# Layer 0 of a four-layer graph network: update and normalization of finished rows as steps of a scheduled list

## The chip, the cores and the metric

The kernel runs on one core of a Trainium2 chip. The metric is the device time of one execution in microseconds (us). The engines are called as the profile calls them: PE (TensorE), DVE (VectorE), ACT (ScalarE), POOL (GpSimd), SP (SyncE, which issues most DMAs); PEld is PE's loading of weights.

## The reference, cut to what matters

Four graph layers, each followed by a residual and a layer normalization. Only layer 0 is changed. N = 2708 nodes, D = 128; `adj` is 2708 x 2708, symmetric in its pattern and about 2.3% dense.

```python
def _L0_gnn_ref(node_feats, adj, msg_w, msg_b, upd_w, upd_b, ln_w, ln_b):
    s = node_feats @ msg_w[:, :D].T
    d = node_feats @ msg_w[:, D:].T
    messages = gelu(s[:, None, :] + d[None, :, :] + msg_b)       # exact gelu
    aggregated = jnp.einsum('ijd,ij->id', messages, adj)
    combined = jnp.concatenate([node_feats, aggregated], axis=-1)
    new_feats = combined @ upd_w.T + upd_b
    h = gelu(new_feats) + node_feats
    mu, var = jnp.mean(h, -1, keepdims=True), jnp.var(h, -1, keepdims=True)
    return (h - mu) / jnp.sqrt(var + LN_EPS) * ln_w + ln_b
...
x = _layernorm(x + _L0_gnn_ref(x, adj, ...))   # layer 0
x = _layernorm(x + _L1_gnn_ref(x, adj, adj, ...))
x = _layernorm(x + _L2_gnn_ref(x, adj, ...))
x = _layernorm(x + _L3_gnn_ref(x, adj, ...))
```

So each row of layer 0's result needs the aggregate of that row, one product with the second half of `upd_w`, a gelu, and two normalizations in a row. Every row is independent of the others.

## The kernel before, in words

Layer 0 does not compute all pairs. For each row tile of 125 rows (22 of them, `Rows`) and each of 22 column blocks of up to 124 columns, it finds the nonzero entries of `adj`: a mask on DVE, ranks by a product with a triangular matrix on PE, and 0/1 matrices `S` on DVE, one for each rank up to five. A block then is: `begin` and `pick` on PE (gather s + d and the weights by products with `S` into a bank `sl`), a gelu on ACT into `g`, the weights `W` on DVE (`weigh`), and `add_up` on PE, which sums weighted messages into the bank `acc`. There are 484 blocks. Entries beyond rank five are "far": DVE finds their places (`max`, `max_index`), POOL gathers rows of a table by indirect DMA (L992, 14 for each row tile), ACT applies gelu and weights to them, and DVE adds them to `extra`. When a row tile is through, `turn` on PE and `close` on ACT write its aggregate, transposed, into columns of `aggT`. `aggT` held x transposed until layer 0's products with x were made.

All of this is a list of steps. `Order.add` takes an engine, an estimated cost, what a step reads and writes, and a due time in blocks (table `DUE`). `Order.run` walks a clock and on each engine takes, of the steps whose inputs are there, the one due first; a step of another kind than the last one on PE counts as due `STAY` blocks later, which keeps alike products together. The order that comes out is each engine's program; on the chip each engine runs it in order and waits where an input is missing. `prepare` (the tables of s, d and of u, which is x's part of the update, stored in `u_tab`) belongs to the same list. One PSUM bank, `misc`, is taken and given back by the steps that need it (ranks, `turn`).

After the list the rest of layer 0 is written out by hand (class `Update` and the lines behind `order.run`): one load of all of u into `o` (`load`, L1156); in groups of four tiles of 128 rows the product with `upd_a` (L1167), the add, gelu (L1169), the residual (L1174), `moments` (L417) and POOL's x + ln_b (L1176); then `Resnorm`: in two halves of 11 tiles, `normalizer` (small operations of 128x11 on DVE and a square root on ACT, L365), a scaling of each tile (`shift`: ACT L455, DVE L457), the product with ln_w (L474), the residual (L475), statistics again, a second `normalizer` and scaling. ACT's square root needs another table than gelu, which costs a table load. Layer 1 then transposes x (L1353), and multiplies it (L1356, L1365, L1359).

Of the kernel before, what the change touches and what calls it, by code (L numbers as in the profile page):

```python
# [15 lines left out]
F32 = mybir.dt.float32  # L16
BF16 = mybir.dt.bfloat16
U32 = mybir.dt.uint32
AF = mybir.ActivationFunctionType
ALU = mybir.AluOpType  # L20
AX = mybir.AxisListType
# [2 lines left out]
P = 128  # L24
BANK = 512
# [12 lines left out]
def spans(start, stop, step):  # L38
    return [(a, min(a + step, stop)) for a in range(start, stop, step)]
# [41 lines left out]
class Order:  # L81
# [4 lines left out]

    LATENCY, TURN, STAY = 0.12, 0.1, 42.0

    def __init__(self):
        self.steps, self.wrote, self.read = [], {}, {}
# [156 lines left out]
def gnn_stack(ctx: ExitStack, tc: tile.TileContext, t, out: bass.AP):  # L249
# [164 lines left out]
    def moments(st, src, a, b):  # L414

        for i in range(a, b):
            nc.vector.bn_stats(out=st[:, i, :], in_=src[:, i, :])  # L417
# [100 lines left out]
    def sums(dst, a, b, r, terms, psum, bias):  # L518

        ps = psum.tile([P, BANK // D, D], F32, name="ps")  # L520
        for i in range(a, b):
            for k, (src, w) in enumerate(terms):
                nc.tensor.matmul(ps[:r, i - a, :], src[:, i * P:i * P + r], w,  # L523
                                 start=k == 0, stop=k == len(terms) - 1)
        nc.vector.tensor_tensor(dst, ps[:r, :b - a, :], over_tiles(bias, b - a, r), op=ALU.add)  # L525
# [103 lines left out]
    with ExitStack() as l0:  # L629
# [10 lines left out]
        with ExitStack() as msg:  # L640
# [79 lines left out]
            def columns_of(sl, a, b):  # L720
# [4 lines left out]

            xT = aggT
            order = Order()
            DUE = {"piece": 0, "spread": -10, "s_out": 23.5, "d_out": 37, "u": 25, "load": -125, "load_s": 94.5,
                   "load_row": -58.5, "start_far": 206, "rank": -20, "rank_row": -18.5, "begin": -1.8, "pick": 0.5,
                   "add_up": 3, "turn": 34.5, "out": 57.5, "cast": -58.5, "a_hi": 21, "gelu": -9.5, "far_weigh": 97.5,  # L730
                   "close": 113.5, "far_gelu": 106, "weigh": -63.5, "largest": -8.5, "index": -35, "mask": -10,
                   "far_sum": -34, "past": -77, "max": -4.5, "a_lo": -12, "S": 4, "fetch": 211}
            add = order.add
            assert NC == 5 and NB % 4 == 2

# [116 lines left out]
            class Rows:  # L852
# [111 lines left out]
                def add_far(self, first):  # L964
# [11 lines left out]
                    for n in range(NOV):  # L976
# [12 lines left out]
                        for k in range(min(8, OV - 8 * n)):  # L989

                            def fetch(k=k, far=far, ix=ix):
# [4 lines left out]
                            add("POOL", 1.95, fetch, due + DUE["fetch"] + k,  # L996
                                reads=[("ix", f), ("far", f), *(("d_tab", j) for j in range(6))],
                                writes=[("far", f, k)], lag=4.0)
                        if t == LT - 1 and n == NOV - 1:
                            break  # L1000
                        self.add_far_gelu(n, f, due)
                    if t < LT - 1:
                        add_, tail = add, self.far_sums(fars)
                        for engine, cost, emit, reads, writes in tail:
                            add_(engine, cost, emit, first + DUE["far_sum"], reads=reads, writes=writes)
                    self.fars = fars

                def add_far_gelu(self, n, f, due):
                    w = min(8, OV - 8 * n)
# [28 lines left out]
                def add_turn(self, due):  # L1038
                    one = ("misc", self.t, "turn")
                    add("PE", 0.85, self.turn, due + DUE["turn"], reads=[("extra", self.t % 2), "agg", "spread"], writes=[one],  # L1040
                        lag=0.08, take="misc", kind="all")
                    add("ACT", 0.2, self.close, due + DUE["close"], reads=[one],
                        writes=[("xT", k) for k in range(len(spans(0, NT, 4)))], give=("misc", one, 1))

                def turn(self):

# [100 lines left out]
                        reads=[("v", t, n) for t in range(LT) for n in range(NOV)]  # L1147
                        + [("count", t, m) for t in range(LT) for m in range(-(-NB // PB))])

            class Update:  # L1150

                def load(self):
                    self.new = o_all[:, :NT * D].rearrange("p (n d) -> p n d", d=D)
                    nc.sync.dma_start(out=self.new, in_=u_tab.rearrange("(n p) d -> p n d", p=P))  # L1156

                def open(self):
                    room, V = (Values.within(g_all[(LT * NB + k) % 6].rearrange("p a d -> p (a d)")) for k in range(2))
                    self.st = room.part([P, NT, 6])  # L1160
                    self.norm = Resnorm(self.new, x, ln_w, self.st, room.part([P, NT, 6]), V)

                def sums(self, n):
                    a, b, r = groups()[n]
                    g, ps = self.new[:r, a:b, :], sl_all[n % 3][:r, n // 3 % 2, :].rearrange("p (i d) -> p i d", d=D)
                    for i in range(a, b):
                        nc.tensor.matmul(ps[:, i - a, :], aggT[:, i * P:i * P + r], upd_a, start=True, stop=True)  # L1167
                    nc.vector.tensor_tensor(g, g, ps[:, :b - a, :], op=ALU.add)
                    nc.scalar.activation(g, g, AF.Gelu)  # L1169

                def rows(self, n):
                    a, b, r = groups()[n]
                    g = self.new[:r, a:b, :]
                    nc.vector.tensor_tensor(g, g, x[:r, a:b, :], op=ALU.add)  # L1174
                    moments(self.st, self.new, a, b)
                    nc.gpsimd.tensor_tensor(x[:r, a:b, :], x[:r, a:b, :], over_tiles(ln_b, b - a, r), op=ALU.add)  # L1176

            U = Update()
            turn_x()
            for n in range(len(spans(0, NB, 4))):  # L1180
                prepare(n)
            for n, (engine, load) in enumerate((
                    ("SP", side_by_side), ("SP", lambda: weight("L1_gnn_W_q")), ("SP", lambda: weight("L1_gnn_W_k")),
                    ("SP", lambda: weight("L1_gnn_W_upd", P)), ("SP", lambda: column("L1_gnn_b_msg")),
                    ("SP", lambda: weight("L3_gnn_W")), ("POOL", lambda: across("L1_gnn_gate_bias")),
                    ("POOL", lambda: across("L1_gnn_ln_gamma")), ("POOL", lambda: across("L1_gnn_ln_beta")),
                    ("POOL", lambda: across("L2_gnn_att_b")), ("POOL", lambda: across("L3_gnn_b")))):
                add(engine, 0.55, load, (5 + n) * NB, reads=[("far", 0, 0)])
            R = [Rows(i) for i in range(LT)]
            for row in R:  # L1190
                row.add()
                row.add_blocks()
                if row.t < LT - 1:
                    row.add_turn(row.t * NB)
            add("DVE", 0.2, lambda: nc.vector.tensor_copy(
                spread[:, :, :RG], ident[:, R[-1].used].rearrange("p (c i) -> p c i", c=NC)), (LT - 1) * NB + 10,
                writes=["spread"])
            add("SP", 0.1, U.load, (LT - 1) * NB + 7, reads=[("u_tab", n) for n in range(6)],
                writes=[("o", m) for m in range(-(-NB // PB))], lag=6.0)
            add_check((LT - 1) * NB + 8)  # L1200
            with tc.manual_schedule():
                order.run({"misc": 1})

                def last_gelu():
                    R[-1].far_gelu(NOV - 1)

                def far_sums():
                    for k in range(OV - 8 * (NOV - 1)):
                        R[-1].far_weigh(NOV - 1, k)
                    for _, _, emit, _, _ in R[-1].far_sums(R[-1].fars):  # L1210
                        emit()

                G = len(groups())
                ahead = LR * (LT - 1) // BANK
                U.open()
                for n in range(ahead):
                    U.sums(n)
                    if n > 0:
                        U.rows(n - 1)
                    if n == 1:  # L1220
                        last_gelu()
                    if n == 2:
                        far_sums()
                R[-1].turn()
                R[-1].close()
                U.rows(ahead - 1)

                ones = mp.tile([P, 1], F32, name="ones")
                fine = mp.tile([P, LT], F32, name="fine")
                n_fine = mp.tile([P, 1], F32, name="n_fine")  # L1230
                nc.vector.memset(ones, 1.0)
                nc.vector.tensor_tensor(fine, tot[:, :, 0], tot[:, :, 1], op=ALU.add)
                nc.vector.tensor_tensor(fine, fine, fine, op=ALU.is_equal)
                nc.vector.tensor_reduce(n_fine, fine, AX.X, ALU.add)
                nc.vector.scalar_tensor_tensor(most, most, float(LT), n_fine, op0=ALU.add, op1=ALU.subtract)

                def between():
                    ps = misc
                    nc.tensor.matmul(ps[:1, 0, :1], ones, most, start=True, stop=True)
                    for n in range(ahead, G):  # L1240
                        U.sums(n)
                    nc.vector.tensor_copy(bad_n, ps[:1, 0, :1])
                    for n in range(ahead, G):
                        U.rows(n)

                U.norm.all(between)

    def all_pairs():

# [862 lines left out]
```

## Time and profile before

| | us |
|---|---|
| runs | 1790.2, 1800.12, 1800.02 |
| median | 1800.02 |
| profiled execution: its own time | 1797.42 |
| profiled execution: span from first to last instruction | 1795.6 |
| PE busy | 1531.0 (85%) |
| DVE busy | 1342.2 (75%) |
| ACT busy | 1069.3 (60%) |
| POOL busy | 566.1 (32%) |

All durations come from the one profiled execution. A line of the profile gives a start, a duration, an engine, the line of the kernel, the operation, output<-input by the program's names, and in brackets how long the engine was idle before and what ended that idle time. A busy share is an average over stages with different limits, so the stages have to be read one by one. The profile says of itself that the ends of matmuls are modelled, and that spans on POOL are rough.

### The profile page before, as it was taken

To read this page: it belongs to the slowest core of one execution; us is meant where nothing else is said; L and a number is where in the kernel's file an instruction comes from. 1 tells how busy PE (TensorE), PEld (TensorE's weight loads), DVE (VectorE), ACT (ScalarE), POOL (GpSimd) and SP (SyncE) were. 2 spreads that over 40 slices of the span, in tenths; PEclk is the share of its full clock that TensorE was granted. 3 is DMA by queue.
4 is the path that set the end of the run, shared out by engine and by line. 5 is a ranking of instruction groups with operands and counts; after the bars stand their busy time and mean duration, and the time that the engine had idled before them with its cause. 6 is when DMAs were issued, how large, how long until landed. Compare 5 with 4: busy or idle time off the path is not lost.

```text
span 1795.6 us, 36325 instructions
## 1 busy us (share of the span) xinstructions
PE 1531.0 (85%) x14033; PEld 936.3 (52%) x14033; DVE 1342.2 (75%) x3139; ACT 1069.3 (60%) x1846; POOL 566.1 (32%) x377
## 2 busy tenths in 40 slices
PE   5799999999999999954999993678887994499995
PEld 4577777777777777742444442222222442145442
DVE  6799999999999999965788858658886873851004
ACT  3378788787887878853453435668877743421003
POOL 2187767767777677641000000000000000000000
PEclk8799999999999999976999996679998996599998
DMA  8676776767767677422244400304334546153431
GB/s 188 167 147 137 166 150 145 153 138 168 145 140 163 145 161 151 103 45 93 99 157 153 157 3 0 113 32 145 145 125 139 171 130 266 65 217 124 155 129 33
DMA packets 228917, 236.37 MB, mean 132 GB/s; under 512 B 25522, under 2 KB 213654, under 8 KB 222146
## 3 DMA queue, kind: packets, MB, share of 16 engines
q1 hardware_dynamic: 184030, 213.15, 38.7%
q0 software_dynamic: 44704, 20.80, 9.9%
q8 instruction: 112, 1.84, 0.4%
q14 instruction: 71, 0.58, 0.1%
HBM read 218.74 MB, written 15.15 MB: 130 GB/s over the span
## 4 chain that ended last, share of the span: by engine, by line
PE 38%; DVE 7%; ACT 7%; issue 1%; ACTq 0%; DVEq 0%
PE acc L2009 11%; PE lg L1397 6%; PE acc L1404 6%; PE accV L1737 5%; PE ps L1665 3%; PE accO L1741 2%; PE ps L1720 1%; ACT arena L1671 1%; PE ps L1666 1%; DVE arena L1699 1%; ACT arena L1692 1%; DVE arena L1723 1%; ACT x L455 1%; PE ps L523 1%; PE ps_w L1365 1%
## 5 line engine op out<-in xcount | busy, mean ns | idle before, releaser
L992 POOL DMA_INDIRECT far<-d_tab,ix x308 | 517.1, 1679 | 251.1 <-ACT g L145 157.0
L145 ACT ACTIVATE g<-sl 128x640 f32<-128x640 f32 x484 | 335.8, 708 | 120.6 <-PE sl L1106 93.8
L1106 PE MATMUL sl<-dA,S 124*128 124x153 f16 x4840 | 378.8, 232 | 1.9 <-DVE S L908 1.9
L1106 PEld LDWEIGHTS <-S 124*128 124x128 f16 x4840 | 329.6, 98 | 47.2 <-issue 39.9
L1114 PE MATMUL acc<-g,W 128*32 128x128 f32 x4840 | 162.5, 275 | 0.7 <-DVE W L1123 0.6
L1098 PE MATMUL sl<-s,same 50*128 50x459 f16 (+1 forms) x968 | 144.4, 331 | 15.9 <-DVE W L1123 11.4
L1398 ACT ACTIVATE w<-lg,row_L_gnn_gate_bias 128x512 f32<-128x512 f32 (+1 forms) x132 | 83.5, 636 | 108.2 <-PE lg L1397 107.0
L1123 DVE TENSOR_TENSOR W<-sl,own 128x125 f32<-128x125 f32 x484 | 128.6, 278 | 16.6 <-ACT g L145 14.5
L1114 PEld LDWEIGHTS acc<-g,W 128*32 128x32 f32 x4840 | 125.8, 109 | 22.4 <-issue 10.9
L981 DVE FIND_INDEX8 ix<-v,o 128x8 uint32<-128x2728 f32 x44 | 131.7, 2994 | 0.0
L1652 POOL TENSOR_TENSOR arena<-arena,off 128x128 f32<-128x128 f32 (+1 forms) x22 | 22.2, 1010 | 340.4 <-DMA arena<-in_adjT 266.9
L1737 PE MATMUL accV<-arena,X 128*128 128x512 f32 (+4 forms) x264 | 123.4, 587 | 6.5 <-DVE arena L1703 6.5
L908 DVE TENSOR_SCALAR S<-rk 124x1000 f16<-124x1000 bf16 (+1 forms) x330 | 125.5, 430 | 0.4 <-ACT rk L888 0.4
L1397 PE MATMUL lg<-qT,mT 128*128 128x512 f32 (+2 forms) x264 | 121.2, 547 | 3.7 <-ACT w L1398 3.1
L1404 PE MATMUL acc<-w,both 128*128 128x512 f32 (+2 forms) x264 | 121.2, 547 | 0.0
L525 DVE TENSOR_TENSOR g<-ps,row_L_gnn_b 128x512 f32<-128x512 f32 (+2 forms) x14 | 8.0, 574 | 147.1 <-PE ps L523 147.1
L1665 PE MATMUL ps<-XT 128*128 128x512 f32 (+8 forms) x150 | 84.1, 647 | 32.2 <-ACT arena L1671 26.5
L2009 PE MATMUL acc<-at,x 128*128 128x512 f32 (+2 forms) x156 | 66.2, 574 | 48.5 <-ACT x L455 48.5
L1022 ACT ACTIVATE far<-far,v 128x128 f32<-128x128 f32 x308 | 104.1, 406 | 0.0
L927 DVE SCALAR_TENSOR_TENSOR o<-misc,ar 128x496 f32<-128x496 f32 x132 | 82.6, 626 | 28.0 <-PE misc L923 13.0
L1399 DVE TENSOR_TENSOR w<-w,at 128x512 f32<-128x512 f32 (+1 forms) x132 | 82.6, 625 | 27.1 <-ACT w L1398 27.1
L888 ACT CAST rk<-misc 124x512 bf16<-124x512 f32 x132 | 72.2, 547 | 44.8 <-PE misc L885 44.2
(359 smaller groups left out, 2502.7 us busy)
## 6 DMA issues: line engine op xcount, KB each, us to landing
at<-in_adjT SPq DMA_DIRECT2D x42, 1354.0 KB
ar<-in_adj SPq DMA_DIRECT2D x110, 248.0 KB
far<-s_tab SPq DMA_DIRECT2D x44, 512.0 KB
at<-in_adjT SPq DMA_DIRECT2D x44, 448.0 KB
arena<-in_adjT SPq DMA_DIRECT2D x21, 704.0 KB
arena<-in_adjT SPq DMA_DIRECT2D x21, 650.0 KB
held<-in_adjT SPq DMA_DIRECT2D x7, 1354.0 KB
f_tab<-arena SPq DMA_DIRECT2D x10, 704.0 KB
```

The source lines that it names most:

```text
L145: s.emit()
L981: add("DVE", 3.0, lambda n=n, ix=ix: nc.vector.max_index(ix, v[:, n * 8:n * 8 + 8], o_all[:, :NB * JB]), due + DUE["index"], reads=[("v", ...
L992: nc.gpsimd.indirect_dma_start(out=far[:, k, :], out_offset=None, in_=d_tab[:, :], in_offset=bass.IndirectOffsetOnAxis(ap=ix[:, k:k + 1], ...
L1098: nc.tensor.matmul(columns_of(sl, 0, DA)[:, a:e, :], same[p], self.s3[p, :e - a, :], start=True, stop=False)
L1106: nc.tensor.matmul(columns_of(sl, 0, DA)[:, c, :], S_all[h][:, n, c, :], dA[q][:, b, c, :], start=False, stop=q == 1 and c in (2, NC - 1))
L1114: nc.tensor.matmul(acc_all[q:q + 32, k, :], W_all[W][:, c, :], g_all[g][:, c, :], start=b == 0 and k == 0, stop=ends)
L1123: nc.vector.tensor_tensor(W[:, :, :RG], columns_of(sl, D, DA), own[:, None, :].to_broadcast([P, NC, RG]), op=ALU.mult)
L1397: nc.tensor.matmul(lg, mT[:, j * P:j * P + r], qT[:, a:b], start=True, stop=True)
L1404: nc.tensor.matmul(acc[k], mrow[:rows[j], j, :], ws[j][:rows[j], a:b], start=j == 0, stop=j == NT - 1)
L1665: nc.tensor.matmul(ps, XT[:, self.js], XT[:, c], start=True, stop=False)
L1737: nc.tensor.matmul(Pair.acc[0][:, a:b], X[:self.r, self.j, :], self.w_[:, a:b], start=first, stop=last)
L2009: nc.tensor.matmul(acc[k], src[:rows[j], j, :], at[:rows[j], a:b], start=j == order[0], stop=j == order[-1])
```

## The change: what it does

The update and both normalizations become steps of the list, by groups of finished row tiles of 128 rows: tiles 0 to 7 once row tile 8 is through, 8 to 15 after row tile 16, 16 to 19 after 20, 20 and 21 after 21 (`SETTLED`, `settle`). Their data lie in columns of `aggT` that are not in use at that time, u is loaded in four parts, and the products go through `misc`. The reciprocal root comes from an integer estimate on DVE and three Newton steps on POOL (`better`, four small operations each; `offset` is one more), so ACT needs no square root. The product with ln_w moves from DVE to POOL, and all scalings are on ACT. The last row tile's far gelu, far sums, `turn` and `close` and the check (`add_bad`) are steps of the list too. `close` now names only the banks of `aggT` that it writes. The due times of all steps and `STAY` are set anew.

```diff
-    LATENCY, TURN, STAY = 0.12, 0.1, 42.0
+    LATENCY, TURN, STAY = 0.12, 0.1, 64.0
...
-            DUE = {"piece": 0, "spread": -10, "s_out": 23.5, "d_out": 37, "u": 25, "load": -125, "load_s": 94.5,
...
+            DUE = {"piece": -5.5, "spread": -4.5, "s_out": 6, "d_out": 26, "u": 8.5, "settle": 25.5, "load": -145.5,
...
-            class Update:
...
-                def sums(self, n):
...
-                def rows(self, n):
...
+            def settle(a, b, room, few, due):
+                w, name = b - a, ("new", a)
+                area, held = columns(room, w * D)
+                T = area.rearrange("p (n d) -> p n d", d=D)
+                area, more = columns(few, w * 14)
+                st = area[:, :6 * w].rearrange("p (n k) -> p n k", k=6)
+                d, q, m, v, y, o, z, u = (area[:, k * w:(k + 1) * w] for k in range(6, 14))
+                even, odd, m2, m5 = (st[:, :, k] for k in (1, 4, 2, 5))
...
+                def load():
+                    nc.sync.dma_start(out=T, in_=u_tab[a * P:b * P, :].rearrange("(n p) d -> p n d", p=P))
...
+                for i, e, r in pieces:
...
+                    step("PE", 1.07 * share, sums, reads=[("xT", i * P // BANK)], writes=[one], lag=0.08, take="misc",
+                         kind="all")
+                    step("DVE", 0.1 + 0.5 * share, lambda t=t, ps=ps, r=r: tt(t[:r], t[:r], ps[:r], op=ALU.add), reads=[one],
+                         writes=[key], give=("misc", one, 1))
+                    step("ACT", 0.1 + 0.5 * share, lambda t=t: nc.scalar.activation(t, t, AF.Gelu), writes=[key])
+                    step("DVE", 0.1 + 0.5 * share, lambda t=t, i=i, e=e: tt(t, t, x[:, i:e, :], op=ALU.add),
+                         reads=[("x", i)], writes=[key])
+                    step("POOL", 0.1 + 1.2 * share, lambda i=i, e=e: nc.gpsimd.tensor_tensor(
+                        x[:, i:e, :], x[:, i:e, :], over_tiles(ln_b, e - i), op=ALU.add), writes=[("x", i)])
...
+                def rates():
+                    r, off = y, o
+                    def begin():
+                        tt(d, even, odd, op=ALU.subtract)
+                        stt(q, d, 0.25, d, op0=ALU.mult, op1=ALU.mult)
+                        stt(m, m2, LN_EPS * D, m5, op0=ALU.add, op1=ALU.add)
+                        stt(u, even, -1.0, odd, op0=ALU.mult, op1=ALU.subtract)
+                    def guess():
+                        stt(v, m, 1.0 / D, q, op0=ALU.mult, op1=ALU.add)
+                        nc.vector.tensor_scalar(y.bitcast(I32), v.bitcast(I32), -0.5, float(0x5f3759df), op0=ALU.mult,
+                                                op1=ALU.add)
+                        nc.vector.tensor_scalar(u, u, 0.5, None, op0=ALU.mult)
+                    def better():
+                        nc.gpsimd.tensor_tensor(z, v, y, op=ALU.mult)
+                        nc.gpsimd.tensor_tensor(z, z, y, op=ALU.mult)
+                        nc.gpsimd.tensor_scalar(z, z, -0.5, 1.5, op0=ALU.mult, op1=ALU.add)
+                        nc.gpsimd.tensor_tensor(y, z, y, op=ALU.mult)
...
+                    step("DVE", 0.7, begin, writes=[(name, "st"), *keys])
+                    step("DVE", 0.5, guess, writes=[(name, "st")])
+                    for _ in range(3):
+                        step("POOL", 0.9, better, writes=[(name, "st")])
+                    step("POOL", 0.25, offset, writes=[(name, "st"), *keys])
+                def scale(src, i, e, key):
+                    for k in range(i, e, 2):
...
+                        step("ACT", 0.39 * min(2, e - k), shift, reads=[(name, "st")], writes=[key])
+                for i, e, _ in pieces:
+                    look(lambda c: T[:, c - a, :], i, e, (name, i))
+                rates()
+                for i, e, _ in pieces:
+                    t, share = T[:, i - a:e - a, :], (e - i) / 4
+                    scale(lambda c: T[:, c - a, :], i, e, (name, i))
+                    step("POOL", 0.1 + 1.2 * share, lambda t=t, i=i, e=e: nc.gpsimd.tensor_tensor(
+                        t, t, over_tiles(ln_w, e - i), op=ALU.mult), writes=[(name, i)])
+                    step("DVE", 0.1 + 0.5 * share, lambda t=t, i=i, e=e: tt(x[:, i:e, :], x[:, i:e, :], t, op=ALU.add),
+                         reads=[(name, i)], writes=[("x", i)])
+                    look(lambda c: x[:, c, :], i, e, ("x", i))
+                rates()
+                for i, e, _ in pieces:
+                    scale(lambda c: x[:, c, :], i, e, ("x", i))
...
+            SETTLED = {8: (0, 8, 3 * BANK, 5 * BANK), 16: (8, 16, 0, 5 * BANK), 20: (16, 20, 2 * BANK, 0),
+                       21: (20, NT, BANK, BANK + 2 * P)}
             for row in R:
                 row.add()
                 row.add_blocks()
...
+                row.add_turn(row.t * NB)
+                if row.t in SETTLED:
+                    settle(*SETTLED[row.t], (row.t + 1) * NB + DUE["settle"])
...
             with tc.manual_schedule():
                 order.run({"misc": 1})
...
-                U.norm.all(between)
```

`look` emits the statistics (`bn_stats`) of two tiles as one step on DVE; the due time of each step in `settle` is 0.1 block later than that of the one before it.

## The prediction

> **What bounds the kernel now.** I cut the span into stages with the table of busy time by stretch:
>
> ```profile
> core 0: us, PE busy (x) PEld busy (x) DVE busy (x) ACT busy (x) POOL busy (x), PEclk, DMA share, GB/s
> 0.00:66.00 66.00, 33.59 (x176) 27.05 (x176) 41.45 (x81) 19.14 (x31) 11.82 (x34) 0.71 0.83 206
> ...
> 300.00:500.00 200.00, 195.89 (x3180) 153.76 (x3178) 189.29 (x477) 161.86 (x325) 145.29 (x86) 1.00 0.70 148
> ...
> 782.00:833.20 51.20, 8.64 (x62) 7.05 (x54) 39.08 (x136) 22.58 (x54) 7.23 (x7) 0.57 0.01 1
> ```
>
> From 66 to 782 us the list of row tiles runs: 484 blocks in 716 us, 1.48 us each. PE is 98% busy and sets the pace, but DVE is at 95%: two engines are nearly full, and ACT is at 81%. From 782 to 833 PE does 8.6 us of work in 51: the update and the normalizations. Then the timeline of that gap:
>
> ```profile
> 782.19 4.73 PE L1167 MATMUL sl<-w_L_upd_wT,aggT 128*128 128x128 f32 x40
> ...
> 796.10 1.13 DVE L1174 TENSOR_TENSOR o<-o,x 128x512 f32<-128x512 f32 x1
> ...
> 797.37 1.26 POOL L1176 TENSOR_TENSOR x<-x,row_L_gnn_ln_b 128x512 f32<-128x512 f32 x1 [0.69 <-DVE o L1174]
> 798.06 0.61 DVE L1232 TENSOR_TENSOR fine<-tot 128x22 f32<-128x22 f32 x1
> ...
> 830.81 2.42 ACT L455 ACTIVATE x<-x,g 128x128 f32<-128x128 f32 x6 [1.23 <-DVE g L444]
> ```
>
> The last scaling ends at 833.24; layer 1 can't start before it. The start of the run, as the timeline has it, has three DVE waits on stores of u:
>
> ```profile
> 55.03 0.69 DVE L820 TENSOR_TENSOR g<-acc,row_L_gnn_upd_b 128x512 f32<-128x512 f32 x1 [4.16 <-DMA u_tab<-g]
> 61.56 0.69 DVE L820 TENSOR_TENSOR g<-acc,row_L_gnn_upd_b 128x512 f32<-128x512 f32 x1 [3.64 <-DMA u_tab<-g]
> 64.39 0.27 DVE L774 MEMSET g<- 128x256 f32 x1 [2.14 <-DMA u_tab<-g]
> 66.08 3.46 PE L1106 MATMUL sl<-dA,S 124*128 124x153 f16 x30 [1.91 <-DVE S L908]
> ```
>
> The profiled execution took 1797.42 us (span 1795.6), 2.6 under the median of three, 1800.02. My sum is made against 1797.4. About 1% (18 us) is what a measurement of this kernel can tell from no change.
>
> **Part 1, the new due times at the start: -4 us.** The order of DVE's instructions shows three of the u sums moved forward, between the sums of s. Their stores go out earlier, so the waits of 4.16, 3.64 and 2.14 us shrink. But the memset of the last u group now stands in front of the first mask (place 60 to the mask's 63; before, the mask was 59th and the memset 74th), and it waits for the third u store, SP's 58th. SP's load of far rows, now 57th, was issued at 45.64; with two more stores of 0.5 us ahead of it the third u store goes at about 47.2. It takes as long as the earlier one (51.64 to 55.03), so the memset comes at 50.6. Behind it stand, by their rows, 0.42 + 0.69 + 0.69 + 1.19 + 0.47 + 0.69 + 1.19 + 2 x 1.56 + 1.8 (five S) = 10.3 us, and about 1 us of waits: first pick at 62 in place of 66.1. Bounds: -9 if all three waits go, +2 if the memset waits longer than I think.
>
> **Part 2, PE's added work beside the list: +7.** Twenty of the 22 update tiles move into the list. They cost 4.73 us for 20 (the x40 line). PE also pays for each change of kind: picks x30 and x20 stand 2.12 and 1.45 us from start to start, so 0.067 us each and 0.11 a group. Counting the order of PE, its changes of kind go from 979 to 1003, 24 x 0.11 = 2.6. PE is the full engine, nothing hides it: +7.3. Bounds +5 to +10.
>
> **Part 3, DVE's added work: mostly hidden, +6.** For eight tiles: six wide operations of 0.69, 16 statistics of 0.22, 14 small ones of about 0.17 (the 128x11 rows) = 4.1 + 3.5 + 2.3 = 9.9 us. Two such settlements lie in the list (weights 224 to 242 and 400 to 418), and 3.4 us of the third, 23 in all. DVE idles only 5%, 1.7 us a row tile, so 9.9 us is hidden by lead, not by idle time. The order shows that lead: the S of the third that starts at block 250 are complete at weight 237 before and at weight 245 after. Eight blocks x 1.48 = 12 us are given up for 9.9. If that cover were gone, PE would wait for S, and all 23 us would be on the path. ACT takes 8 scalings in a row (8 x 0.39 = 3.1 us), ahead of the gelu that PE's next bank waits for; PE has about two blocks in hand. I take 2.5 us for each big settlement and 1 for the third. Bounds 0 (nothing is taken off DVE or ACT in the list, so no gain) and 23. SP's one load of u becomes four, the first in front of the second row tile's columns; issues of 0.4 to 0.7 us for loads that are due some 145 blocks ahead, so nothing.
>
> DVE and POOL also get in each other's way. At 796.10 an add that takes 0.69 elsewhere takes 1.13 and ends after POOL's; at 798.06 one of 0.17 takes 0.61. The other side is POOL's row in layer 2:
>
> ```profile
> L1652 POOL TENSOR_TENSOR arena<-arena,off 128x128 f32<-128x128 f32 x21 | 22.0, 1048 | 328.7 <-DMA arena<-in_adjT 266.9 <-issue 51.8 <-DVE arena L1723 10.0
> ...
> L1176 POOL TENSOR_TENSOR x<-x,row_L_gnn_ln_b 128x128 f32<-128x128 f32 x1 | 0.5, 455 | 11.9 <-DVE o L1174 11.9
> ...
> L1652 POOL TENSOR_TENSOR arena<-arena,off 20x20 f32<-20x20 f32 x1 | 0.2, 217 | 11.7 <-PE ps L1720 11.7
> ```
>
> The same shape takes 0.46 us free and 1.05 beside DVE. The Trainium skill has the rule behind this ("SBUF — State Buffer", section "Who interferes with whom"): a DVE operation with two SBUF inputs, or in a two-port mode, and a GpSimd operation that reads SBUF exclude each other for a whole instruction. It speaks against this change: some 40% of DVE's time in the list is of such kinds, and ten wide POOL operations of 1.27 us come in. That share is L903, L908, L878 and L1031, 285 us of 716; no run shows how often they meet POOL there. By the rule DVE would lose about 10 x 1.27 x 0.4 = 5 us more, and the sum below would be -8 instead of -13.
>
> **Part 4, the end: -22.** Count from the last sum (782.26 before). Before: 51.0 us to 833.24, then 2.9 to layer 1's first product (836.18). After, along the order: DVE's second look at tiles 16 to 19 stands behind the last weight, which ends 0.7 before that sum, and takes 0.69 + 0.87 + 1.2, so it ends 2.1 after; Newton steps and offset on POOL (13 operations, N); four scalings 1.6; gelu and six weights of the last far rows 2.7, queued on ACT behind those scalings; DVE's far sums 2.4; turn 1.6 and close 0.3; two update tiles through one bank with gelu, add and statistics 3.7; N; scalings 0.8, POOL product 0.9, add and statistics 0.6, small ones 1.2; N; scalings 0.8. That is 18.7, plus 15 handovers of 0.1, plus 3N. All three table loads of 1.28 us are gone, since no root is left on ACT. The trace has no small dependent POOL chain. Lower bound of one operation: the 20x20 row, 0.22 us. Upper: that plus the 0.30 us between POOL's gathers, 0.52. I take 0.28, near the row of the same size, since each step waits only for its own engine: N = 3.6, the end 31.1. Layer 1's transposes lie beside it, 0.8 to the first product. 53.9 - 31.9 = 22. Bounds: -24 at 0.22, -13 at 0.52.
>
> **Sum:** -4 + 7 + 6 - 22 = -13, that is 1784 us, 0.9% under the median.
>
> **Rivals.** (a) *The list has no cost and the start no waits*: -8 + 7 + 0 - 22 = -23, 1774. For it: the order keeps lead, and three u waits are visible; against it: DVE at 95%. (b) *DVE becomes the bound*: the lead in the order isn't there in time, all 23 us are paid: -4 + 7 + 23 - 22 = +4, 1801, no gain. For it: 42.6 us of DVE work in 34 us of blocks; against it: PE waits only 11.4 us for DVE's weights in the whole list. (c) *The Newton chain is late for ACT*, slower than before. Place: the scalings stand four blocks, about 6 us, behind DVE's guess in ACT's queue, in front of the gelus. Price: under DVE's load one operation is 0.52 + (1.05 - 0.46) = 1.11 us, a chain 14.4, 8.4 late; five chains in the list, less 1.5 us of gelu in hand each, 35; the end then gains 13: -4 + 7 + 6 + 35 - 13 = +31, 1828. The chain is late from 0.46 us an operation, and the whole is slower from about 0.59. Against it: the 0.22 row, and that 8 of the 22 POOL products of layer 2 keep 0.46 although DVE is busy there. That the roots stay on ACT is excluded by the order: no table load is left there between gelus.
>
> **Chances.** Forecast 0.50 (1777 to 1791), (a) 0.18, (b) 0.22, (c) 0.10. The range 1772 to 1806 leaves out (c) and little of (a). Faster than 1782: all of (a) and four tenths of the forecast, 0.38; slower by over 1%: (c), 0.10; between them 0.52.
>
> **What would show it.** First pick near 62 us; last sum near 791 (782 - 4 + 13); layer 1's first product some 32 us after that; POOL's small operations at 0.28 us from start to start; PE's waits on DVE S or on ACT near blocks 224 to 250 and 400 to 426 below 3 us each. Newton chains over 6 us with ACT idle before its scalings would prove me wrong by (c), waits of PE for S by (b).

## The result, and the profile after

The changed kernel takes 1805.89 us (median of 22 runs, 1800.32 to 1816.65), the kernel before in the same series 1799.78: ratio 1.0054, 95% interval 1.0036 to 1.0072. So it is half a percent slower, where 0.9% faster was forecast. The profiled execution took 1800.32 us, 2.9 more than that of the kernel before; it is the fastest of the 22, and the medians are 6.1 us apart, so the profile accounts for about half of the difference and the rest stays open. Cut into stages, the table of busy time by stretch reads now (start and end, then length, then busy time and instructions of each engine, the granted clock, the DMA share and rate):

```profile
core 0: us, PE busy (x) PEld busy (x) DVE busy (x) ACT busy (x) POOL busy (x), PEclk, DMA share, GB/s
62.64:394.00 331.36, 321.68 (x5211) 251.41 (x5213) 312.86 (x801) 262.14 (x515) 238.34 (x140) 1.00 0.72 152
394.00:472.74 78.74, 69.86 (x1060) 53.97 (x1056) 73.90 (x194) 59.79 (x124) 59.27 (x58) 0.96 0.59 130
472.74:664.77 192.03, 189.58 (x3117) 148.84 (x3112) 183.27 (x470) 156.60 (x314) 141.81 (x84) 1.00 0.73 153
664.77:743.26 78.49, 70.22 (x1068) 54.42 (x1060) 74.58 (x193) 59.88 (x124) 60.85 (x58) 0.96 0.60 130
743.26:804.83 61.57, 60.01 (x987) 46.56 (x980) 50.79 (x138) 47.07 (x97) 47.65 (x41) 1.00 0.39 71
804.83:840.00 35.17, 6.16 (x24) 4.58 (x24) 10.96 (x49) 8.09 (x23) 16.17 (x48) 0.56 0.34 124
```

The second and the fourth row are the two big settlements. Their bounds are DVE's weights 220 to 264 and 396 to 440, 44 blocks each. The same blocks of the kernel before:

```profile
399.19:464.55 65.36, 63.68 (x1046) 50.11 (x1038) 61.66 (x158) 52.17 (x105) 48.20 (x28) 1.00 0.72 150
657.69:722.31 64.62, 63.57 (x1044) 49.93 (x1040) 61.25 (x157) 52.41 (x106) 46.15 (x28) 1.00 0.73 152
```

Each settlement makes its 44 blocks 13.4 and 13.9 us longer; DVE is busy 12.2 and 13.3 us more. Elsewhere the list is as before: -1.8 us up to block 220, -1.1 between the settlements, +1.6 after the second. Sum: the list went from 716.2 to 742.2 us, +26. PE doesn't wait for S in it but for the weights W that stand behind the new work in DVE's queue (PE's largest wait in the list: its total in us, how often, the longest one; the same pair was 11.4 us in 22 waits before):

```profile
PE sl L1096 <- DVE W L1121: 23.0, 30, 2.2
```

The timeline at the start, and around the end:

```profile
62.64 2.69 PE L1104 MATMUL sl<-dA,S 124*128 124x153 f16 x20
...
804.20 0.63 PE L1112 MATMUL acc<-g,W 128*32 128x128 f32 x12 [0.40 <-DVE W L1121]
...
808.49 0.81 POOL L1236 TENSOR_TENSOR aggT<-aggT 128x4 f32<-128x4 f32 x1
809.38 0.20 POOL L1237 TENSOR_TENSOR aggT<-aggT 128x4 f32<-128x4 f32 x1
809.67 0.19 POOL L1238 TENSOR_SCALAR aggT<-aggT 128x4 f32<-128x4 f32 x1
809.94 0.20 POOL L1239 TENSOR_TENSOR aggT<-aggT 128x4 f32<-128x4 f32 x1
...
836.03 0.88 ACT L1256 ACTIVATE x<-x,aggT 128x128 f32<-128x128 f32 x2 [6.03 <-POOL aggT L1242]
837.00 0.49 DVE L1400 COPY wT<-ps 128x128 f32<-128x128 f32 x2 [4.51 <-ACT x L1256]
...
840.03 2.07 PE L1413 MATMUL ps_m<-xT,w_both 128*128 128x512 f32 x2
```

First pick 3.4 us earlier, last sum at 804.83 where 782.26 was, layer 1's first product 35.2 us behind it where it was 53.9: -3.4 + 26.0 - 18.7 = +3.9, and 840.03 stands against 836.18. POOL's small operations at the end are 0.28 us apart, after a first one of 0.81.

What follows layer 1's first product isn't touched by the change, yet it takes 959 us in some profiled executions and 970 in others. So below I read lists and ends from the stages and not from the span. Lists of the same order also differ by a few us outside the settlements from one execution to another; what a settlement costs is therefore read from the two stretches of 44 blocks.

### The profile page after: what moved, and what is told of

The parts are those of the page before. It is cut to its first block, busy times and chain, and to the rows that moved or that the text cites. A ratio compares the mean times of both kernels' runs of the same rounds, so it can differ in the third digit from the quotient of the medians.

```text
span 1798.6 us, 36428 instructions
## 1 busy us (share of the span) xinstructions
PE 1534.4 (85%) x14033; PEld 935.6 (52%) x14033; DVE 1340.4 (75%) x3134; ACT 1069.9 (59%) x1855; POOL 602.8 (34%) x488
## 4 chain that ended last, share of the span: by engine, by line
PE 38%; DVE 8%; ACT 6%; issue 1%; ACTq 0%; DVEq 0%
PE acc L2066 11%; PE lg L1454 6%; PE acc L1461 5%; PE accV L1794 5%; PE ps L1722 3%; PE accO L1798 2%; PE ps L1777 1%; ACT arena L1728 1%; DVE arena L1756 1%; PE ps L1723 1%; DVE arena L1780 1%; PE ps L524 1%; ACT x L456 1%; PE ps_w L1422 1%; ACT arena L1749 1%
## 5 line engine op out<-in xcount | busy, mean ns | idle before, releaser
L1112 PE MATMUL acc<-g,W 128*32 128x128 f32 x4840 | 167.0, 278 | 2.1 <-DVE W L1121 2.0
L1112 PEld LDWEIGHTS acc<-g,W 128*32 128x32 f32 x4840 | 126.8, 110 | 26.6 <-issue 13.3
L910 DVE TENSOR_SCALAR S<-rk 124x1000 f16<-124x1000 bf16 (+1 forms) x330 | 130.5, 444 | 0.3 <-PE sl L1104 0.3
```

Source lines behind the costliest of these rows:

```text
L910: add("DVE", 0.06 + 0.27 * share, lambda k=k: nc.vector.tensor_scalar(S_all[h][:, :n, :, k * RG:(k + 1) * RG], ranks, EDGE + k, None, op0= ...
L1112: nc.tensor.matmul(acc_all[q:q + 32, k, :], W_all[W][:, c, :], g_all[g][:, c, :], start=b == 0 and k == 0, stop=ends)
```

## The experiments

**Is it the settlements, or the new order?** The two big ones left out:

```diff
-                if row.t in SETTLED:
+                if row.t in (20, 21):
```

> The changed kernel, with the settlements of tiles 0 to 7 and 8 to 15 left out (their update and normalizations aren't computed); the last six tiles are settled as before. The list of row tiles (first pick to last sum) took 716.2 us in the kernel before and 742.2 in the changed one, and its lateness grew only in blocks 220 to 253 (+14.0 us) and 396 to 429 (+13.5). Theory 'work': both steps are the settlements themselves, so the list comes back to 742.2 - 27.5 = 715 us, within 2. Rival 'order': the new due times place the row tiles' own steps worse near those blocks; then the list stays above 725.

List 715.8 us, and the 44 blocks (columns as above):

```profile
395.39:459.66 64.27, 63.50 (x1040) 49.56 (x1034) 61.07 (x157) 52.20 (x105) 47.37 (x28) 1.00 0.73 152
653.61:717.72 64.11, 63.31 (x1040) 49.59 (x1034) 60.95 (x157) 51.93 (x105) 46.68 (x28) 1.00 0.72 153
```

The new due times cost nothing; a settlement costs 78.7 - 64.2, some 14.4 us by its own order, and that is the whole loss. DVE is busy 12.8 and 13.6 us less here; only the other 1.6 and 0.8 us are added idle time of DVE. (Ratio 0.988 to the kernel before, with that work missing.)

**Is DVE full there?** The statistics doubled (the edit below), and, in another kernel, four wide adds and half of the statistics of each big settlement left out where they stand:

```diff
+                                if w == 8:
+                                    nc.vector.bn_stats(out=st[:, c - a, :], in_=src(c))
```

> The changed kernel, with each of the 16 statistics of each big settlement issued twice (same operands, same result): 16 x 0.28 = 4.5 us of DVE work more in each of the two settlements, and nothing else moved. Theory 'DVE full': in those stretches DVE is busy 94% and has nothing to hide work in, so it is all paid: list 742.2 + 9 = 751 us. Rival 'ACT burst': half of each settlement's cost comes from ACT's eight scalings of x in a row, which hold up the gelus while DVE waits; then DVE has idle time there and the list grows by 4 us or less, to 746 at most.

The 44 blocks:

```profile
397.36:480.87 83.51, 70.13 (x1067) 54.11 (x1060) 78.02 (x210) 60.02 (x124) 58.77 (x58) 0.96 0.57 123
675.28:758.79 83.51, 72.84 (x1070) 56.52 (x1064) 79.28 (x210) 59.98 (x124) 60.38 (x58) 0.92 0.56 122
```

They are 4.8 and 5.0 us longer for 4.5 us of work: paid in full, with no idle DVE to take it. (The list is 758.1, 6 us above what the two explain; 3 of these arose ahead of block 220, and why is open.) Ratio 1.0052 (1.0020 to 1.0084).

> The changed kernel, order unchanged, with 4 wide adds (0.68 us) and 8 of the 16 statistics (0.28 us) of each big settlement left out: 5.0 us less of DVE work in each. Theory 'DVE full': a DVE microsecond in a settlement costs a microsecond of the list (doubled statistics cost 4.8 and 5.0 us for 4.5), so the list is 742.2 - 10 = 732 us. Rival 'ACT burst': the stall behind the eight scalings is untouched, so only the other half of each settlement shrinks; list 737 or more.

Stretches 75.29 and 76.29, list 737.6: 3.5 and 2.2 us saved of 5.0. That is less than expected, and a list that the rival had named (737 or more), so this run doesn't tell the two apart; the rival is tried by itself next. DVE's busy time fell by only 2.4 and 2.5 us, and the rows of S say what came in between: the 124x750 steps took 554 ns in the mean, where they take 371 in the changed kernel. One of them, at 411.20 us, took 2.26 us beside POOL's second addition. With other work taken away, other steps stood beside POOL's wide operations. That leads to POOL, below.

**Is it ACT's eight scalings in a row?** From 437 to 440 us ACT scales eight tiles of x in a row, the gelus are late, and PE almost stops (1.13 us of work in 4); its granted clock then shows 0.50:

```profile
440.00:444.00 4.00, 1.13 (x12) 0.84 (x12) 2.88 (x4) 4.00 (x10) 3.39 (x3) 1.00 0.27 33
444.00:446.00 2.00, 1.21 (x6) 0.36 (x5) 2.00 (x7) 1.97 (x5) 1.69 (x2) 0.50 0.32 39
446.00:450.00 4.00, 4.00 (x55) 3.45 (x55) 2.51 (x6) 1.55 (x6) 3.39 (x3) 0.50 0.84 180
```

It looks like half of the cost. First the scalings were spread by due times, then left out where they stand:

```diff
+                turn = itertools.count()
-                        step("ACT", ..., writes=[key])
+                        step("ACT", ..., writes=[key], k=4 * next(turn))
```

> The changed kernel, with the due times of ACT's scalings spread, so that the eight scalings of x stand as 2, 4 and 2 with a gelu between them, where they were 8 in a row (3.2 us); all else in the list keeps its place nearly. Theory 'ACT burst': the late gelus leave PE almost idle for 5 us (at 440 and at 713 us), and PE's granted clock then shows 0.5 for some 5 us more: about 7 of each settlement's 13.7 us. With the burst broken up most of that goes: list 742.2 - 12 = 730 us, and no clock of 0.5 near blocks 250 and 426. Rival 'DVE full': what is paid is DVE's 12 us of work for each settlement, wherever ACT puts its scalings: list 740 to 742.

The list got longer, 749.3 us (ratio 1.0086, 1.0067 to 1.0106). In blocks 242 to 253 the run lost 1.0 us against the kernel before, where the changed kernel lost 7.8, so the stall was gone from there; its stretches of 44 blocks were 74.39 and 74.67. But by block 308 it had lost 14.0 us since block 220, the changed kernel 13.3. The planner had moved other steps as well, up to row tile 15, so this alone doesn't decide it. The next one does for the burst:

```diff
-                            for c in range(k, n):
+                            for c in range(k, n) if w < 8 or key[0] != "x" else ():
```

> The changed kernel, order unchanged, with ACT's eight scalings of x in a row left out in each big settlement (3.2 us each). In the run where the planner had broken up the burst, PE's stall after it was gone, but the planner had also moved other steps for four row tiles, and the list was no shorter; here the order is that of the changed kernel. Theory 'DVE full': DVE's queue has as much to do as before, list 740 to 742 us. Rival 'ACT burst': without the burst no stall at 440 and 713 us, list 742.2 - 12 = 730 us. In between would mean that the stall is a cost of its own, on top of DVE's work.

Stretches 78.46 and 80.05, list 744.2. So the burst is not the cause: without it a settlement costs as much. But the stall and the half clock didn't go with it: from 442 to 447 us PE did 2.01 us of work while DVE was busy 4.96, and the mean granted clock of the two stretches was 0.96 and 0.94, where it is 0.96 and 0.96 in the changed kernel. What the half clock costs of its own is thus not shown. In the changed kernel DVE waits for a product of PE in it:

```profile
448.97 0.67 DVE L929 SCALAR_TENSOR_TENSOR o<-misc,ar 128x496 f32<-128x496 f32 x1 [1.49 <-PE misc L925]
```

As DVE idles only 1.6 and 0.8 us more than without a settlement, an estimate from these rows is that such waits cost no more than that.

**Can the work be spread over idle time?**

```diff
-                    add(engine, cost, emit, due + next(at) * 0.1 + k, ...)
+                    add(engine, cost, emit, due + next(at) * 6 + k, ...)
```

> The changed kernel, with the steps of a settlement due 6 blocks apart instead of 0.1, so that the planner lays one big settlement over some 75 blocks where it took 20. The work is the same. Outside the settlements DVE idles 4% of a row tile, 1.3 us of 32.5, so 75 blocks offer 4 to 5 us of idle DVE time to each settlement, and ACT's bursts are 4 scalings at most. Theory 'DVE full' alone: a settlement costs 12 less 4 to 5, list 742.2 - 10 = 732. With the ACT burst as a second cause as well: another 12 less, list 720 to 724. If spreading brings nothing (the cost is in PE's or POOL's own work), the list stays at 740 to 744.

It got worse: list 759.5, ratio 1.0086 (1.0053 to 1.0120). About half of it isn't the settlement's own work: between the two, where nothing of a settlement is left (blocks 330 to 352), a row tile takes 34.30 us with DVE idle 3.2, where it took 31.98 with DVE idle 1.4. The order of a row's own steps hadn't come back: the S of a row's last third are now complete as soon as DVE has done the weights of the row tile before, 11 weights earlier than in the changed kernel. The order is found step by step from its due times, and a disturbance can settle it in another cycle; that this cycle is what makes the row tile longer is argued, not tested. What spreading would bring in an undisturbed order stays open.

**Does POOL hold DVE up?** POOL's four wide operations of each big settlement left out (x plus ln_b, T times ln_w):

```diff
-                    step("POOL", ..., lambda ...: nc.gpsimd.tensor_tensor(
+                    step("POOL", ..., lambda ...: w < 8 and nc.gpsimd.tensor_tensor(
```

> The changed kernel, order unchanged, with POOL's four wide operations (1.7 to 1.9 us each) left out in each big settlement. In the settlements DVE's S steps took 535 ns in the mean instead of 432 and its far sums 718 instead of 587, some 3.3 us for each settlement. Theory 'POOL holds DVE up': these go back to their free durations, list 742.2 - 6.6 = 735.5 us. Rival: the longer DVE steps have another reason (what POOL's gathers do to them, say), list 741 to 742 and S stays near 535 ns there.

List 734.0, and the 44 blocks are 4.8 and 5.0 us shorter, more than expected:

```profile
395.11:469.08 73.97, 68.53 (x1062) 52.73 (x1056) 69.32 (x193) 59.53 (x124) 54.59 (x54) 0.95 0.66 139
662.43:735.91 73.48, 68.17 (x1071) 52.59 (x1060) 69.33 (x193) 59.75 (x124) 56.52 (x54) 0.98 0.66 139
```

S, by form, blocks 220 to 264, first the changed kernel (count, then busy time in us and mean ns of one):

```profile
L910 DVE TENSOR_SCALAR S<-rk 124x1000 f16<-124x1000 bf16 x20 | 11.2, 598 | 0.0
```

and without POOL's operations:

```profile
L910 DVE TENSOR_SCALAR S<-rk 124x1000 f16<-124x1000 bf16 x20 | 7.7, 424 | 0.0
```

One place of the changed kernel's timeline holds 2.8 of the 3.5 us:

```profile
421.44 3.10 POOL L1267 TENSOR_TENSOR aggT<-aggT,row_L_gnn_ln_w 128x512 f32<-128x512 f32 x2
421.65 3.20 DVE L910 TENSOR_SCALAR S<-rk 124x1000 f16<-124x1000 bf16 x1
```

One S step of 0.42 us takes 3.20, until both products of POOL are over (3.19 in the second settlement). The far sum beside the first addition is the other: 0.69 us free, 1.73 and 2.40 in the two settlements. To tell this from shorter waits for POOL, the same four operations were issued on DVE:

```diff
-                    step("POOL", ..., lambda ...: nc.gpsimd.tensor_tensor(
+                    step("POOL", ..., lambda ...: (tt if w == 8 else nc.gpsimd.tensor_tensor)(
```

> The changed kernel, with POOL's four wide operations of each big settlement (x plus ln_b, T times ln_w, 128x512 each) issued on DVE at the same places, 0.68 us each there; nothing is left out. Without them the list was 8.2 us shorter (734.0 for 742.2), 4.9 us a settlement. Theory 'a wide POOL operation holds DVE up': POOL's four cost DVE more than doing them itself, 4.9 against 4 x 0.68 = 2.7 us, so the list gets shorter by about 4, to 738 us, and the S steps there take 430 ns again. Rival 'DVE only has more to do': the 8.2 us came from shorter waits for POOL's results, and 5.4 us of DVE work is added to a full engine: list 745 to 748.

Stretches 75.88 and 75.85: 2.9 and 2.7 us shorter, though DVE does 2.7 us more. S takes 426 ns again. Measured against the run without them, the four operations cost a settlement 4.8 and 5.0 us on POOL, and 1.9 and 2.4 on DVE. The whole list was 741.6, between the two expectations: 3.0 us were lost between the settlements and 1.9 ahead of them, where nothing differs, and why is open. Ratio 1.0036 (1.0008 to 1.0064).

**So where does the work belong?** DVE is full in the list and free behind it. All settlements behind the list, still with Newton steps on GpSimd; tiles 0 to 19 as one group, u in the index search's array:

```diff
-            SETTLED = {8: (0, 8, ...), 16: (8, 16, ...), 20: (16, 20, ...), 21: (20, NT, ...)}
+            add("SP", 0.1, load_u, (LT - 1) * NB + 7, ..., writes=[("o", m) ...], lag=6.0)
+            settle(20, NT, 0, 0, LT * NB + DUE["settle"])
+            settle(0, 20, 0, 0, LT * NB + DUE["settle"] + 10)
...
-                    step("PE", 1.07 * share, sums, reads=[("xT", i * P // BANK)], ...)
+                    step("PE", 1.07 * share, sums, reads=[("xT", i * P // BANK), ("S", len(thirds) - 1, CAP - 1)], ...)
...
+                        if k % 4 and w > 8:
+                            step("DVE", 0.25 * min(2, e - k), shift_, reads=[(name, "st")], writes=[key])
```

> All settlements behind the list, the roots still by Newton steps on GpSimd: tiles 0 to 19 are one group and tiles 20 and 21 a second, their u rows lie in the index search's array, the update's matmuls wait for the last S step of the list, POOL's part waits for the last fetch, and DVE takes half of the group's scalings. Theory 'DVE full': in the list a settlement's work costs its full time, at the end DVE, ACT and PE are idle. List 716.2 + 3.5 for PE's update matmuls = 720 us, the stretch from the last sum to layer 1's first product 28 to 32 us (35.2 in the changed kernel, 53.9 in the kernel before): 62.6 + 720 + 30 = 813 us where the changed kernel has 840 and the kernel before 836; some 23 us faster than before, ratio 0.987. Rival: the end then becomes bound by POOL's Newton steps and wide operations or by DVE, 45 us or more, and the ratio is 0.995 or above.

The list was 716.4 us, PE's 20 update products in its last blocks hidden or nearly so; the end 47.8, so the rival was right on the end: ratio 0.9995 (0.9973 to 1.0018). DVE's adds waited for POOL's additions, the last of which ended at 812.9 us. With these on DVE:

```diff
-                    step("POOL", 0.1 + 1.2 * share, lambda i=i, e=e: nc.gpsimd.tensor_tensor(
+                    step("DVE", 0.1 + 0.5 * share, lambda i=i, e=e: tt(
```

> All settlements behind the list, as in the run before it (list 716.4 us, but 47.8 us from the last sum to layer 1's first product), with x plus ln_b taken from POOL to DVE. There POOL was the chain's bound: five wide additions of 1.3 to 2.9 us stood between its Newton steps and DVE's adds waited for them until 814. If POOL's queue was the bound, the first group's adds end near 797, its second Newton chain at 801 and its last scalings near 805, where they ended at 824.7: the stretch is 28 to 33 us, layer 1's first product comes at 810 to 814 us and the ratio to the kernel before is 0.986 to 0.99. If DVE is the next bound (33 us of its work lie there), the stretch is 40 us and the ratio 0.995.

End 40.7, list 715.5, ratio 0.9934 (0.9909 to 0.9960). POOL's queue was part of it; the second theory named the end (40) rightly. Then the large group ahead of the small one, whose roots went to DVE:

```diff
-                        nc.gpsimd.tensor_tensor(z, v, y, op=ALU.mult)
+                        on.tensor_tensor(z, v, y, op=ALU.mult)
...
+                    root, on = ("POOL", nc.gpsimd) if w > 8 else ("DVE", nc.vector)
```

> As the run with all settlements behind the list and x plus ln_b on DVE (715.5 us of list, 40.7 us of end, ratio 0.993 to the kernel before), with two edits: the group of tiles 0 to 19 goes ahead of tiles 20 and 21 on every engine, and the small group's roots are taken on DVE. There POOL's fifth product stood behind the small group's second Newton chain, and the large group's own second chain began at 808.9 us. If POOL's queue was the bound, the large group's second chain now begins near 799 and its last scalings end near 806: an end of 30 to 33 us, layer 1's first product at 809 to 812 us, ratio 0.987 to 0.989. If the small group (its gelu stands behind ten scalings on ACT now) becomes the last, the end stays at 36 to 40 us and the ratio at 0.991 to 0.994.

End 40.8, ratio 0.9914 (0.9885 to 0.9944). The table says why the end didn't move: DVE is busy 19.2 of its first 20.4 us.

```profile
62.34:777.60 715.26, 702.22 (x11410) 551.08 (x11408) 675.13 (x1734) 571.89 (x1133) 518.84 (x308) 1.00 0.70 147
777.60:798.00 20.40, 3.87 (x14) 2.48 (x14) 19.23 (x56) 6.73 (x23) 11.82 (x18) 0.59 0.00 0
```

Last, the scalings of T back to ACT, all roots on GpSimd, the small group's first half ahead:

```diff
-                        if k % 4 and w > 8:
+                        if key[0] == "x" and k % 4 and w > 8:
...
+                due += 10 * (w < 8)
```

> As the runs with all settlements behind the list. In the last one DVE was busy 97% of the first 20 us of the end (it had taken scalings of T, 0.6 us each beside POOL's products where two of them cost 0.58 alone, and the small group's roots). Here ACT, which was busy 10 of 35 us, takes all scalings of T, the roots of both groups are on GpSimd, and the small group's first half goes ahead of the large group, its second half behind. If DVE was the bound, the large group's adds end near 799, its second chain near 804.5 and the last scalings near 809: layer 1's first product at 811 to 813 us where it came at 818.4, an end of 34 us, ratio 0.986 to 0.989 to the kernel before. If ACT's 22 scalings in a row (8.9 us) or POOL's queue take DVE's place, the end stays at 38 to 41 us and the ratio at 0.991 to 0.994.

Ratio 0.9895 (0.9861 to 0.9928), the end 37.4 us, between the two expectations: now POOL does six products in a row (7.1 us) and DVE's adds wait for them again. This execution's list was 721.7, some 6 us above the others of its order. The intervals of the last three ratios overlap, so which of them is best isn't shown; each beats the kernel before, the last by 1.05%, and by way of its ratio of 1.0054 the changed kernel too.

## Why the prediction was wrong

**Part 1 was right.** First pick at 62.64 (62 predicted), -3.4 for -4: the three waits became one of 5.79 us, and the memset came at 51.74 for 50.6. And leaving the settlements out gave 715.8 us of list, so the rest of the new order is neutral.

**Part 3 was the step that failed.** It put 2.5 us on each big settlement, on the ground that 12 us of lead are given up for 9.9 us of DVE work. With part 2's 7 us the list was to grow by 13; it grew by 26. The lead was read at one third of one row tile. That one, starting at block 250, is indeed complete 7 or 8 weights later than before. But the order gives, for the next third (block 258), weight 253 in both kernels, and for the row tile after that the lead of the undisturbed rows. The lead was borrowed and given back within one row tile, and DVE's idle time, 1.4 us of 32, can't pay it back. A lead hides work only if it stays given up. The sign of it was in part 3 itself ("If that cover were gone"), but where it named PE's wait for S, PE waits for W: in an in-order queue the new work stands ahead of the next weights, however early S is.

**The price inside it was two prices.** Without POOL's wide operations a settlement's 44 blocks are 73.97 and 73.48 us, 8.6 and 8.9 above the kernel before. DVE is then busy 7.7 and 8.1 us more: this is the work that the prediction put at 9.9, and it is paid in full. POOL's four operations add 4.8 and 5.0. Part 3 weighed just this with the Trainium skill's rule ("SBUF — State Buffer", section "Who interferes with whom"), and left it out of the sum. The rule was right, and 40% was too low a share: eight operations cost 9.8 us, 1.2 each, nearly the whole of the 1.27 us that the prediction gave them. The planner puts three of each four where DVE is at a far sum or S, kinds that the rule names; S and the far sum alone lost 3.8 and 4.5 us.

**Part 2 and part 3 were added, though they compete.** PE's update products are in the list, but in the settlements PE idles 8 to 9 us, so they lie inside the time that DVE takes. When DVE is the bound of a stretch, PE's added work there isn't a term of its own.

**Rival (b) was right in its kind, and in its number partly by luck**: DVE as the bound, 1801 us by it against 1800.32 for the profiled execution. Its 30 us for the list (23 + 7) stand against 26, but they are made up otherwise: no PE term, less DVE work, and 10 us for POOL. What was held against it, that PE waits only 11.4 us for DVE's weights before, says little: PE at 98% and DVE at 95% means that the slack of the second engine is gone after 1.4 us a row tile.

**Part 4 was right in its kind, -18.7 for -22.** At the end a Newton operation takes 0.28 us, as put; the first of a chain 0.81 where DVE is at work. Two terms were too small. Layer 1's first product comes 3.1 us after the last scaling, not 0.8, because its weight copies (L1400 at 837.00) wait for that scaling instead of lying beside the end: 2.3 us. And tiles 16 to 19 are done 9.5 us after the last sum (at 814.33), where the terms give 7.5 (2.1 for DVE's look, 3.6 for the roots, 1.6 for four scalings, handovers): DVE's look ended 0.7 later, and POOL's chain began 0.9 behind it and took 4.2. The far gelu of the last rows is queued on ACT behind these scalings, as put, so 2 us more. The rest of the chain came out 1 us shorter. Rival (c) fell: the chains in the big settlements took 5.2 to 5.7 us for 3.6, ACT idled 1.3 us at most before its scalings there, and with the scalings of x left out, which wait for the second chain, the list was no shorter.

## What to carry to other kernels

Two engines at 98% and 95% were one bound here: the work moved into that stretch was paid in full, and the place to look for cover is a stretch where engines are idle, here the end. Before a lead is counted as cover, follow it until the order is back in its usual cycle; if the lead is back, the work was paid. And a wide elementwise operation handed to GpSimd is not off DVE's path: here four of them cost 4.9 us, and 2.1 when DVE did them itself.

## What the runs showed of the hardware

One DVE step can wait through several POOL operations: S, 0.42 us alone, took 3.20 beside two back-to-back products of POOL, so DVE wasn't served between them. Two other kinds pass untouched. Beside POOL's addition, statistics (0.28 us each in the mean of the settlement) and a weight (0.28), whose other input is in PSUM, keep their usual times:

```profile
410.33 0.49 DVE L1215 BATCH_NORM_STATS2 aggT<-aggT 128x6 f32<-128x128 f32 x2
410.44 1.28 POOL L1207 TENSOR_TENSOR x<-x,row_L_gnn_ln_b 128x512 f32<-128x512 f32 x1 [1.54 <-DVE aggT L1205]
410.73 0.27 DVE L1121 TENSOR_TENSOR W<-sl,own 128x125 f32<-128x125 f32 x1
```

That is how the rule named above divides the kinds: at most one SBUF input and no two-port mode doesn't contend. Scalings by DVE's TENSOR_SCALAR follow it too: ten took 2.65 us with POOL idle, six took 3.60 when POOL's products came in beside them. And PE's granted clock fell to 0.50 after some 4 to 5 us in which PE was nearly idle (1.13 us of work from 440 to 444 us), and was back some 7 us later (0.80 in the mean from 450 to 452, 1.00 from there); what that costs was not measured by itself.
